# Pairs of tiles in the prefix counts, weights by head at unit ends, and loads, copies and transposes moved between queues and engines in a four-layer graph kernel

## The chip, the cores and the metric

The kernel runs on one core of one Trainium2 chip. The metric is the time of one execution on the device in microseconds (us), the median of the runs shown. The core has these engines: PE (matrix products, with its weight loads shown as PEld), DVE (vector), ACT (scalar functions), POOL (GpSimd), and SP, which only issues transfers. Each engine works off its own instructions in order. Transfers are issued from queues of SP, ACT or POOL and run on 16 DMA engines.

## The reference

A graph of 3327 nodes with 512 features passes through four layers. After each one, x becomes the layer norm of x plus the layer's result. Layers 0, 2 and 3 are graph attention, with 8, 8 and 4 heads; layer 1 takes the mean over the first 64 neighbours of each row.

```python
# attention (layer 0; layers 2 and 3 the same with an elu behind)
Wh = einsum('ni,hio->hno', h, W);  f1 = Wh . a1;  f2 = Wh . a2
e  = leaky_relu(f1[:, :, None] + f2[:, None, :], 0.2)
attention = softmax(where(adj > 0, e, -9e15), axis=-1)
h_prime = einsum('hnm,hmo->hno', attention, Wh)
# layer 1 (sage)
keep    = (A > 0) & (cumsum(A > 0, axis=1) <= 64)
nb_mean = keep @ X / max(keep.sum(1), 1)
out     = leaky_relu(X @ W_line.T + b_line) + where(cnt > 0, leaky_relu(nb_mean @ W_nb.T + b_nb), 0)
```

## The kernel before

Nodes are cut into NT = 26 tiles of 128. The transposed adjacency lies in on-chip memory as `mask`, one byte per entry, 128 x 26 x 3328. The instructions of PE are in the order in which they are written; those of the other engines are ordered by a planner, except where `tc.keep_in_program_order` pins one.

**Projection.** For each tile, `project1` transposes x on PE and `project2` multiplies with the weights, which yields the values and, in 2H extra columns, f1 and f2. ACT copies these to `fc` (L269), DVE scales the values (L271), and they go to DRAM as `v`. In layer 0 the projection runs beside the loading of the mask: 104 pieces of up to 416 KB (`mask_steps`), of which `EARLY` = 88 are loaded and set here and the rest in the first units of attention. `prepare` (L293) and `cut` (L317) turn f1 and f2 of one half of the tiles into exponentials, rows in DRAM (`rd`) and bf16 pieces; for the second half they are jobs of the first attention unit.

**Attention.** A softmax weight is a maximum of two products of exponentials, so a weight tile `t` is one DVE instruction: the larger of a row `rb` and a column, times the mask (L402). ACT makes from it an fp8 tile `y` that tells which side won (L405). PE multiplies `t` with the values into four accumulators `po` (L411) and `y` and the mask with small coefficient columns into `pd`, the denominators (L371). Target nodes go in two halves of 1664 columns, heads in NS = 4 slots: a `unit` (L358) is one half and one slot, with HS = 2 heads in layers 0 and 2 and one in layer 3, and loops over the 26 source tiles j:

```python
for k, h in enumerate(heads):
    t = tp.tile([P, IW], F32, name="t")          # 3 * HS buffers
    nc.vector.scalar_tensor_tensor(t, rb[k], self.qc[:, j, h:h + 1], ...)
```

Rows come by POOL's queue (L350, a pool of 3 buffers, so one row of the next unit can come early and the other only after a row of this unit was last read), values `vj` by SP's queue, two tiles at a time, in four buffers. At a unit's end `po` is copied to `ob`, its first part by DVE (L429) and three by ACT (L427). PE transposes `ob` in four groups of up to four blocks (`transposed`, L435) during the next unit, one job per j; each group is copied to `hb` (by ACT, in layer 3 by DVE, L443) and stored to `hd` on SP's queue. After the last slot of a half `pd` is copied to `db` (L458 ACT, L459 DVE); the job `reciprocals` sums it on PE (L466) and divides on DVE (L474 to L477).

**Between layers** `finish` loads rows of `hd` (SP's queue) and of the layer's input (POOL's queue), two tiles at a time, and does division, sum and norm; the first two tiles come before the next layer's loop (`ending`).

**Sage.** A first part (L623, L626) multiplies each tile with two weight matrices. In the second part, target nodes go in 13 blocks of 256. For each block and each of the 26 source tiles `kept` makes the tile `kt`: ACT copies the count carried in from the tiles before into a PSUM tile (`carry_in`, L694), PE adds the running count inside the tile by a triangular matrix (L702), DVE compares with 64 and multiplies with the mask (L706). There are two such PSUM tiles, 128 x 256 each. PE then adds three products per source tile into `acc` (L734); while one block is summed the `kt` of the next are made, up to 11 tiles ahead. Carries come as `cy`, four tiles at a time, by POOL's queue (L592). Finished tiles are normed (ACT: square root, identity) and projected for layer 2 (ACT: exponential).

**Layer 3's second half** holds its output in `g` and does elu, statistics and norm as slots end (`final`), with the last of it behind the last unit.

## Time and profile before

| | |
|---|---|
| median of 3 runs | 3477.88 us (3473.75 to 3479.80) |
| profiled execution, its own time | 3476.22 us |
| span of its instructions | 3474.4 us |
| mean clock granted to PE | 0.983 |
| busy: PE, DVE, ACT, POOL | 3320.6, 2699.8, 2387.0, 213.3 us |
| L402 (weight tiles, DVE) | 1040 instructions, 1944 ns each |
| L405 (ACT) | 1040, 1766 ns each |
| L706, L694, L702 (prefix counts) | 338 each: 420, 374, 273 ns |

| stage | from, about (us) |
|---|---|
| projection of layer 0, mask loads | 0 |
| attention of layer 0, 8 units | 156 |
| sage, first part; second part | 985; 1190 |
| attention of layer 2, 8 units | 1820 |
| projection of layer 3 | 2615 |
| attention of layer 3, 8 units; its end | 2765; 3440 |

Lengths of single instructions overlap at their ends: back to back, instructions start closer together than the length of one, so a rate is read from starts. A time line's row gives start, length (of a group of neighbours), engine, line, tiles and, in brackets, the idle time before it and what ended it. A row of the waits gives who waited for what, total us, times, longest.

### The profile page before, as it was taken

The numbers are of one execution on the slowest core, as the hardware profiler recorded it, in microseconds if no ns is written. First come the engines' busy times: TensorE is split into PE (matmuls) and PEld (weight loads), VectorE is DVE, ScalarE is ACT, GpSimd is POOL, SyncE is SP. The second block draws the span as 40 slices with busy tenths as digits, with TensorE's granted clock in tenths as the row PEclk, the third lists the DMA queues.
The fourth block names the chain that finished last, engine by engine and source line by source line (L and its number), as shares of the span: only waits on it lengthen the run. The fifth ranks groups of instructions, "written<-read, shape, count | busy, mean of one in ns | idle before, by whom it ended". The sixth has DMA issues, their size and how long they took to land.

```text
span 3474.4 us, 48117 instructions
## 1 busy us (share of the span) xinstructions
PE 3320.6 (96%) x18873; PEld 1700.4 (49%) x18926; DVE 2699.8 (78%) x2771; ACT 2387.0 (69%) x2324; POOL 213.3 (6%) x340
## 2 busy tenths in 40 slices
PE   8799999999989999999989999999998999999997
PEld 6544444444444455545554444444446655555553
DVE  6699999999957544344349999999997766668886
ACT  1388988999953343443328999899997655558885
POOL 3100000000010111111110000000001000000000
PEclk9899999999989999999999999999999999999998
DMA  9722111110133422222220111111106511112211
GB/s 382 284 86 68 50 48 47 47 49 28 37 121 122 136 82 68 75 67 69 73 78 18 48 49 47 51 46 43 39 28 205 176 33 44 40 46 91 83 37 47
DMA packets 205354, 276.67 MB, mean 80 GB/s; under 512 B 19325, under 2 KB 140359, under 8 KB 205128
## 3 DMA queue, kind: packets, MB, share of 16 engines
q1 hardware_dynamic: 173464, 164.97, 14.5%
q0 software_dynamic: 26720, 102.65, 9.3%
q10 hardware_dynamic: 4944, 5.98, 0.5%
q8 instruction: 149, 2.44, 0.3%
q14 instruction: 77, 0.63, 0.1%
HBM read 204.92 MB, written 68.60 MB: 79 GB/s over the span
## 4 chain that ended last, share of the span: by engine, by line
PE 59%; issue 27%; DVE 6%; DMA 5%; ACT 2%; POOL 1%; ACTq 0%; POOLq 0%; SPq 0%; DVEq 0%
PE po L411 33%; PE acc L734 9%; PE pd L371 4%; PE pw L265 4%; DVE t L402 3%; DMA raw<-in_adjT_dram 3%; PE pz L623 3%; PE pi L626 2%; PE pt L435 1%; ACT y L405 1%; DMA cy<-ctd 1%; PE pk L702 1%; DVE kt L706 1%; PE pe L466 1%; PE pt L254 1%
## 5 line engine op out<-in xcount | busy, mean ns | idle before, releaser
L402 DVE SCALAR_TENSOR_TENSOR t<-rb,qc,mask 128x1664 f32<-128x1664 f32 x1040 | 1959.5, 1944 | 191.7 <-PE po L411 154.4
L405 ACT ACTIVATE y<-t,bi,sc 128x1664 fp8e4<-128x1664 f32 x1040 | 1771.6, 1766 | 339.1 <-PE pd L371 324.5
L411 PE MATMUL po<-t,vj 128*64 128x448 f32 (+3 forms) x8320 | 1934.8, 521 | 23.8 <-DVE t L402 23.5
L411 PEld LDWEIGHTS po<-t,vj 128*64 128x64 f32 (+1 forms) x8320 | 856.4, 148 | 972.8 <-issue 676.3
L734 PE MATMUL acc<-zs,kt 128*128 128x512 bf16 x1314 | 394.7, 380 | 1.5
L265 PE MATMUL pw<-wsb,xT 128*128 128x264 f32 (+1 forms) x1248 | 301.8, 397 | 18.6 <-DVE vt L271 15.6
L734 PEld LDWEIGHTS <-kt 128*128 128x128 fp8e4 x2028 | 198.2, 98 | 226.4 <-issue 29.8
L694 ACT CAST pk<-cy 128x256 f32<-128x256 bf16 x338 | 124.0, 374 | 268.2 <-DVE kt L706 220.5
L265 PEld LDWEIGHTS pw<-wsb,xT 128*128 128x128 f32 x1248 | 240.7, 197 | 62.9 <-issue 14.1
L371 PE MATMUL pd<-y,sden 128*32 128x448 fp8e4 (+1 forms) x4160 | 259.7, 342 | 10.5 <-ACT y L405 10.5
L706 DVE SCALAR_TENSOR_TENSOR kt<-pk,mask 128x256 fp8e4<-128x256 f32 x338 | 140.8, 420 | 157.2 <-PE pk L702 156.6
L734 PE MATMUL acc<-zl,kt 128*128 128x512 bf16 x661 | 251.1, 380 | 1.4 <-DMA zl<-zd 0.8
L371 PEld LDWEIGHTS <-sden 128*32 128x32 bf16 x4160 | 117.7, 96 | 162.4 <-issue 139.7
L269 ACT COPY fc<-pw 128x8 f32<-128x8 f32 (+1 forms) x156 | 23.6, 162 | 148.2 <-PE pw L265 148.2
L271 DVE TENSOR_TENSOR vt<-pw,dc 128x256 f32<-128x256 f32 x156 | 58.7, 417 | 80.8 <-ACT dc L266 76.6
L350 POOL DMA_DIRECT2D rb<-r x40 | 21.2, 532 | 1617.0 <-DVE t L402 1610.2
L702 PE MATMUL pk<-mask,upto 128*128 128x256 fp8e4 x338 | 92.3, 273 | 19.9 <-ACT pk L694 18.9
L526 DVE TENSOR_SCALAR mask<-raw 128x832 fp8e4<-128x832 int32 (+2 forms) x98 | 58.4, 603 | 51.0 <-DMA raw<-in_adjT_dram 50.7
L623 PE MATMUL pz<-wn,xT 128*128 128x512 f32 x208 | 96.1, 606 | 1.3 <-ACT xT L617 1.3
L626 PE MATMUL pi<-wl,xT 128*128 128x512 f32 x208 | 93.5, 592 | 0.0
L592 POOL DMA_DIRECT2D cy<-ctd x91 | 67.8, 745 | 395.9 <-ACT pk L694 267.8
L714 DVE SCALAR_TENSOR_TENSOR y<-acc,cnt,bnb 128x512 f32<-128x512 f32 x26 | 19.5, 751 | 83.5 <-PE acc L734 83.5
(167 smaller groups left out, 1750.7 us busy)
## 6 DMA issues: line engine op xcount, KB each, us to landing
vj<-v SPq DMA_DIRECT2D x312, 128.0 KB
rb<-r POOLq DMA_DIRECT2D x40, 832.0 KB, 4.7
raw<-in_adjT_dram SPq DMA_DIRECT2D x71, 416.0 KB
cy<-ctd POOLq DMA_DIRECT2D x78, 256.0 KB, 3.9
h<-hd SPq DMA_DIRECT2D x65, 256.0 KB
hd<-hb SPq DMA_DIRECT2D x60, 256.0 KB
v<-vt SPq DMA_DIRECT2D x50, 256.0 KB
xr<-x POOLq DMA_DIRECT2D x45, 256.0 KB, 3.2
```

Source lines behind the costliest of these rows:

```text
L265: nc.tensor.matmul(pw[e][:, :FW + H], xT[:, c, :], wsb[:, c, e, :], start=c == 0, stop=c == FC - 1)
L371: nc.tensor.matmul(pd[c][32 * kk:32 * kk + 32, :w_], lhsT, rhs, start=(kk, c) not in seen, skip_group_check=final is not None, stop=last a ...
L402: nc.vector.scalar_tensor_tensor(t, rb[k], self.qc[:, j, h:h + 1], mask[:, j, i0:i0 + IW], op0=ALU.max, op1=ALU.mult)
L405: nc.scalar.activation(y, t, AF.Sigmoid, bias=self.bi[:, j, h:h + 1], scale=self.sc[:, j, h:h + 1], saturate=False)
L411: nc.tensor.matmul(po[c][k * D:(k + 1) * D, :z - a_], vj[:, j % 2, k * D:(k + 1) * D], ts[k][:, a_:z], start=j == 0, stop=j == NT - 1)
L592: nc.gpsimd.dma_start(out=cy[:, :n, :], in_=ctd[t:t + n, b * GW:(b + 1) * GW] .rearrange("(o t) i -> o t i", o=1).to_broadcast([P, n, GW]))
L623: nc.tensor.matmul(pz, xT[:, c, :], wn[:, c, :], start=c == 0, stop=c == FC - 1)
L626: nc.tensor.matmul(pi, xT[:, c, :], wl[:, c, :], start=c == 0, stop=c == FC - 1)
L694: nc.scalar.copy(pks[k % 2], carry[b, t // 4 * 4][:, t % 4, :])
L702: nc.tensor.matmul(pk, upto, mask[:, t, i0:i0 + GW], start=False, stop=True, skip_group_check=True)
L706: nc.vector.scalar_tensor_tensor(kt, pk, NEIGHBOURS, mask[:, t, i0:i0 + GW], op0=ALU.is_le, op1=ALU.mult, saturate=False)
L734: nc.tensor.matmul(acc, kts[t][:, s * P:(s + 1) * P], zs(t, c) if c < 2 else zl[:, t, :], start=t == 0 and c == 0, stop=t == NT - 1 and c ...
```

## The change

- `kept` makes two tiles at a time: PSUM tiles of 128 x 2 x 256, one matmul, one ACT copy, one DVE instruction for both; `kt` has half as many buffers of twice the size.
- In units with two heads the weights of the first two and of the last two source tiles are made head by head: (0,0), (1,0), (0,1), (1,1).
- `fc` is gone: f1 and f2 are copied into `rc` and `qc` and worked on in place.
- In layers 0 and 2 all copies of `po` and `pd` are ACT's.
- In layer 3's first half DVE transposes 32 x 32 blocks from PSUM into `ob`, and four transfers per unit put the blocks in place in DRAM, in runs of 32 numbers; the transposes on PE and the copies to `hb` fall away there.
- `reciprocals` is cut in two jobs, the sums on PE and, two tiles later, the division; at the very end the first transposes go ahead of the sums, and tiles are normed and stored in reverse.
- `prepare` and `cut` of the second half come two tiles later in layers 0 and 2, and instructions of theirs are pinned to program order.
- The first `finish` in the loops behind layers 0 and 2 (tiles 2 and 3) loads `hd` by POOL's queue.
- `EARLY` is 82, the first 8 mask pieces (not 4) are issued by ACT's queue, and w0's transposed rows have four buffers instead of three.

```diff
-    def finish_steps(pool, xin, layer, t0, n, hbufs=6):
+    def finish_steps(pool, xin, layer, t0, n, hbufs=6, eng=nc.sync):
...
-                load_tile(h, hd, t, nc.sync)
+                load_tile(h, hd, t, eng)
...
         def columns(self, pool):
...
-            self.fc = pool.tile([P, NT, 2 * H], F32, name=f"fc{li}")
...
-                nc.scalar.copy(self.fc[:, t, e * H:(e + 1) * H], pw[e][:, FW:FW + H])
+                nc.scalar.copy((self.rc, self.qc)[e][:, t, :], pw[e][:, FW:FW + H])
...
-        def prepare(self, pool, half, tag="rr", bufs=2):
+        def prepare(self, pool, half, tag="rr", bufs=2, pinned=False):
...
-            f1, f2 = self.fc[:, ts, :H], self.fc[:, ts, H:]
...
-            nc.vector.tensor_scalar(rc, f1, RCLAMP, -RCLAMP, op0=ALU.min, op1=ALU.max)
+            ins = nc.vector.tensor_scalar(rc, rc, RCLAMP, -RCLAMP, op0=ALU.min, op1=ALU.max)
+            if pinned:
+                tc.keep_in_program_order(ins)
...
-            nc.scalar.activation(qc, f2, AF.Exp, scale=1.0 - ALPHA)
+            nc.scalar.activation(qc, qc, AF.Exp, scale=1.0 - ALPHA)
...
-        def cut(self, pool, half, tag="pc", bufs=1):
+        def cut(self, pool, half, tag="pc", bufs=1, pinned=False):
...
-                nc.vector.tensor_copy(pc[:, :, :, c0], dc)
+                ins = nc.vector.tensor_copy(pc[:, :, :, c0], dc)
+                if pinned:
+                    tc.keep_in_program_order(ins)
...
+            def weights(j, k):
+                h = heads[k]
+                t = tp.tile([P, IW], F32, name="t")
+                nc.vector.scalar_tensor_tensor(t, rb[k], self.qc[:, j, h:h + 1],
+                                               mask[:, j, i0:i0 + IW], op0=ALU.max, op1=ALU.mult)
+                y = yp.tile([P, IW], F8, name="y")
+                nc.scalar.activation(y, t, AF.Sigmoid, bias=self.bi[:, j, h:h + 1],
+                                     scale=self.sc[:, j, h:h + 1], saturate=False)
+                return t, y
...
+                if HS == 1 or j not in (1, NT - 1):
+                    made = {}
+                    for k in range(HS):
+                        for j_ in (j, j + 1) if HS > 1 and j in (0, NT - 2) else (j,):
+                            made[j_, k] = weights(j_, k)
+                ts, ys = zip(*(made[j, k] for k in range(HS)))
...
+            by_dma = HS == 1 and not final
...
-                if c:
+                if by_dma:
...
+                    nc.vector.transpose(ob[:, a_:z], po[c][:, :z - a_])
+                elif c or HS == 2:
...
-                    final(s, s0, n, pt)
-                    return
+                    return final(s, s0, n, pt)
...
-                if HS == 2:
-                    nc.scalar.copy(hb[:, :n], pt[:, :n])
-                else:
-                    nc.vector.tensor_copy(hb[:, :n], pt[:, :n])
+                nc.scalar.copy(hb[:, :n], pt[:, :n])
...
-            for s0, n in QUADS:
-                jobs += [lambda s0=s0, n=n: transposed(s0, n), nothing]
+            if by_dma:
+                for b in range(4):
+                    nc.sync.dma_start(out=hd[i0:i0 + IW, s * P + 32 * b:s * P + 32 * b + 32]
+                                      .rearrange("(q i) f -> i q f", i=32),
+                                      in_=ob[32 * b:32 * b + 32, :].rearrange("p (q f) -> p q f", f=32))
+            else:
+                for s0, n in QUADS:
+                    jobs += [lambda s0=s0, n=n: transposed(s0, n), nothing]
...
-                nc.vector.tensor_copy(db[64:, c * (WB // 2):(c + 1) * (WB // 2)], pd[c][64:, :WB // 2])
...
-            def reciprocals():
-                pe = qp.tile([P, HALF, 2, H], F32, name="pe", tag="q")
+                (nc.scalar.copy if HS == 2 else nc.vector.tensor_copy)(
+                    db[64:, c * (WB // 2):(c + 1) * (WB // 2)], pd[c][64:, :WB // 2])
+            held = []
...
+            def sums():
...
+                pe = po[0][:, :2 * HALF * H].rearrange("p (q o h) -> p q o h", q=HALF, o=2) if final and s == NS - 1 else \
+                    qp.tile([P, HALF, 2, H], F32, name="pe", tag="q")
+                held.append(pe)
...
+            def reciprocals():
+                pe = held[0]
...
-                    nc.vector.tensor_tensor(r_[:, :, k, ss], pv[:, :, 0, k, ss], rc[:, :, k, ss], op=ALU.mult)
+                    tc.keep_in_program_order(
+                        nc.vector.tensor_tensor(r_[:, :, k, ss], pv[:, :, 0, k, ss], rc[:, :, k, ss], op=ALU.mult))
...
-            return jobs[:2] + [reciprocals] + jobs[2:]
+            if final and s == NS - 1:
...
+                take = []
+                return [lambda: take.append(transposed(*QUADS[0])), lambda: take.append(transposed(*QUADS[1])),
+                        sums, reciprocals] + [lambda q=q: take[q]() for q in range(2)] + \
+                    [lambda q=q: transposed(*q)() for q in QUADS[2:]]
+            return jobs[:2] + [sums, nothing, reciprocals] + jobs[2:]
...
-                    ys, ahead = ahead, finish(fp, xin, prev, t0 + 2, 2) if t0 + 2 < NT else None
+                    ys, ahead = ahead, finish(fp, xin, prev, t0 + 2, 2, 6, nc.sync if t0 else nc.gpsimd) \
+                        if t0 + 2 < NT else None
...
-                    tc.tile_pool(name="sb_k", bufs=NT + 10, reuse_waits="tile") as kp, \
+                    tc.tile_pool(name="sb_k", bufs=NT // 2 + 5, reuse_waits="tile") as kp, \
...
-                pks = [pkp.tile([P, GW], F32, name=f"pk{i}") for i in range(2)]
+                pks = [pkp.tile([P, 2, GW], F32, name=f"pk{i}") for i in range(2)]
...
-                    nc.tensor.matmul(pk, upto, mask[:, 0, :GW], start=True, stop=True)
...
-                order = [(b, t) for b in range(len(blocks)) for t in range(NT)]
+                    nc.tensor.matmul(pk, upto, mask[:, 0:2, :GW], start=True, stop=True)
...
+                order = [(b, t) for b in range(len(blocks)) for t in range(0, NT, 2)]
...
                 def carry_in(k):
...
-                        nc.scalar.copy(pks[k % 2], carry[b, t // 4 * 4][:, t % 4, :])
+                        nc.scalar.copy(pks[k % 2], carry[b, t // 4 * 4][:, t % 4:t % 4 + 2, :])
...
                 def kept(b, t):
...
-                    nc.tensor.matmul(pk, upto, mask[:, t, i0:i0 + GW], start=False, stop=True,
+                    nc.tensor.matmul(pk, upto, mask[:, t:t + 2, i0:i0 + GW], start=False, stop=True,
...
-                    kt = kp.tile([P, GW], F8, name="kt")
-                    nc.vector.scalar_tensor_tensor(kt, pk, NEIGHBOURS, mask[:, t, i0:i0 + GW],
+                    kt = kp.tile([P, 2, GW], F8, name="kt")
+                    nc.vector.scalar_tensor_tensor(kt, pk, NEIGHBOURS, mask[:, t:t + 2, i0:i0 + GW],
...
-                    return kt
+                    return [kt[:, 0, :], kt[:, 1, :]]
...
                 def output(acc, t):
...
-                kts = [kept(0, t) for t in range(4)]
+                kts = kept(0, 0) + kept(0, 2)
...
-                            if b == 0 and len(kts) < NT:
-                                kts.append(kept(0, len(kts)))
+                            if b == 0 and len(kts) < NT and t % 2 == 0:
+                                kts += kept(0, len(kts))
...
-                            if not last and (len(ahead) < 10 and t % 2 == 1 and b > 0 if s == 0 else
-                                             len(ahead) < min(NT, t + 11)):
-                                ahead.append(kept(b + 1, len(ahead)))
+                            if not last and (len(ahead) < 10 and t % 4 == 1 and b > 0 if s == 0 else
+                                             len(ahead) < min(NT, t + 10) and t % 2 == 1):
+                                ahead += kept(b + 1, len(ahead))
...
-                    ys, ahead = ahead, finish(fp, x2, L2, t0 + 2, 2) if t0 + 2 < NT else None
+                    ys, ahead = ahead, finish(fp, x2, L2, t0 + 2, 2, 6, nc.sync if t0 else nc.gpsimd) \
+                        if t0 + 2 < NT else None
...
+                    def take():
+                        h = fp.tile([P, 4, P], F32, name="h", bufs=2)
+                        nc.vector.tensor_tensor(h[:, :n], pt[:, :n], rec[:, HALF + q0:HALF + q0 + n, s:s + 1]
...
+                        if s == NS - 1:
...
+                        return take
+                    take()
...
-                    for q in range(qs.start, qs.stop):
+                    for q in reversed(range(qs.start, qs.stop)):
...
+        L0.columns(cp)
...
-            L0.columns(wp)
...
-            EARLY = 3 * NT + 10
-            msteps = mask_steps(rw0, pieces[:EARLY], 5, (), False, 4)
+            EARLY = 3 * NT + 4
+            msteps = mask_steps(rw0, pieces[:EARLY], 5, (), False, 8)
...
             def attend(pool, tag, dst, wT, a, k, held):
...
-                wt = pool.tile([P, F], F32, name="wt", tag=tag)
+                wt = pool.tile([P, F], F32, name="wt", tag=tag, bufs=FC if tag == "wt" else 1)
...
-                return [lambda: L0.prepare(f0, 1, "xr", 1), lambda: L0.cut(f0, 1, "h", 2)] + count_jobs(pool, 0)
+                return [lambda: None] * 2 + [lambda: L0.prepare(f0, 1, "xr", 1, True), lambda: L0.cut(f0, 1, "h", 2, True)] + \
+                    count_jobs(pool, 0)
...
-                L2.attention(rp, lambda pool, half, s: [lambda: L2.prepare(mp, 1, "rr", 1), lambda: L2.cut(mp, 1, "pc", 1)]
+                L2.attention(rp, lambda pool, half, s: [lambda: None] * 2 +
+                             [lambda: L2.prepare(mp, 1, "rr", 1, True), lambda: L2.cut(mp, 1, "pc", 1, True)]
...
```

## The prediction

> **What bounds the kernel now.** First I read slices and windows, to cut the run into stages; then, stage by stage, the time line and the table of waits, to see what each stage is paced by.
>
> From the page, busy tenths in 40 slices of 87 us (PE, DVE, clock granted to PE, DMA):
>
> ```profile
> PE   8799999999989999999989999999998999999997
> DVE  6699999999957544344349999999997766668886
> PEclk9899999999989999999999999999999999999998
> DMA  9722111110133422222220111111106511112211
> ```
>
> PE looks full everywhere, so it can't be what tells the stages apart. The others do: DMA fills only the start (to about 155 us, the projection of layer 0 with the mask loads); DVE is full from 160 to 970 (attention, layer 0) and from 1820 to 2612 (layer 2); only PE is full in the sage layer (985 to 1820) and in layer 3's attention (2765 to 3440).
>
> The time line inside layer 2 (start, length, engine, line):
>
> ```profile
> 1898.68 24.30 DVE L402 SCALAR_TENSOR_TENSOR t<-rb,qc,mask 128x1664 f32<-128x1664 f32 x13
> 1903.11 13.47 ACT L405 ACTIVATE y<-t,bi,sc 128x1664 fp8e4<-128x1664 f32 x8 [1.44 <-PE pd L371]
> 1922.89 0.62 DVE L429 COPY ob<-po 128x448 f32<-128x448 f32 x1
> 1923.88 28.02 DVE L402 SCALAR_TENSOR_TENSOR t<-rb,qc,mask 128x1664 f32<-128x1664 f32 x15 [0.37 <-DMA rb<-r]
> ```
>
> DVE makes a weight tile each 24.30/13 = 1.87 us with nothing between; 52 of them are 97.1 us, and a unit is 98. The rest of a unit is the copy (0.62) and the wait for the next rows (0.37). ACT needs 13.47/8 = 1.68 each, 87.6 a unit, with 8 copies of about 0.5 some 92. PE needs 13 pairs of tiles at 5.83 (32 instructions, where they run unpaced in the chain) and 0.87 for the denominators, 87.1, about 2.8 for the masks' denominators and 1.9 for transposes: 92. So DVE sets these 16 units with 5 us to spare on both others, and only what DVE loses counts there.
>
> The waits of DVE, first in layer 0 (160 to 985), then in layer 2 (1820 to 2615): total, times, longest:
>
> ```profile
> DVE t L402 <- DMA rb<-r: 3.2, 4, 1.6
> DVE rec L474 <- PE pe L466: 2.7, 1, 2.7
> ...
> DVE t L402 <- DMA rb<-r: 2.5, 4, 0.8
> DVE rec L474 <- PE pe L466: 2.4, 1, 2.4
> ```
>
> The sage layer's second part (1190 to 1820): PE waits for ACT's carry copies, by the table of waits and by one place on the time line:
>
> ```profile
> PE pk L702 <- ACT pk L694: 18.9, 20, 1.9
> ...
> 1319.37 1.28 ACT L154 ACT_TABLE_LOAD   x1
> 1319.94 0.38 PE L734 MATMUL acc<-zl,kt 128*128 128x512 bf16 x1
> 1321.28 0.27 PE L702 MATMUL pk<-mask,upto 128*128 128x256 fp8e4 x1 [0.96 <-ACT pk L694]
> ```
>
> Start to start that is 1.34 us where 0.215 is normal: a table load on ACT holds up the one tile of lead.
>
> Two more places: the end of layer 0, and a transpose in layer 3.
>
> ```profile
> 992.28 2.77 SPq L126 DMA_DIRECT2D h<-hd  x6
> 1005.25 1.12 PE L615 MATMUL pt<-ident,h 128*128 128x128 f32 x4 [5.75 <-ACT h L161]
> ...
> 2857.63 0.60 PE L435 MATMUL pt<-ident,ob 128*128 128x128 f32 x4
> 2858.06 2.96 PE L411 MATMUL po<-t,vj 128*128 128x448 f32 x8
> ```
>
> **The change, part by part.** The sum is against the profiled execution's own time, 3476.22 us (span 3474.4 and 1.8 around it), 1.7 under the median 3477.88.
>
> *Start.* Six mask pieces of 416 KB leave the DMA-bound start: 2.56 MB at the 370 to 390 GB/s of its rows is 6.7 us. They come back in layer 0's first units, 3 on ACT, 3 on DVE at 0.59: +1.8. A fourth buffer for w0's transposed rows and four more raw loads on ACT's queue move bytes about in a full DMA: 0. Pinning the second half's preparation takes some 7 us of small DVE work from before the first weight tile (156.0) to after it; DVE is full there, so 0 net. It also puts its two Exp between Sigmoids: two table loads of 1.28 on ACT (cover: ACT's 5 us a unit), and PE, in written order, waits at the preparation's transposes for clamp and Exp. DVE has six tiles of lead, 11 us. Before, 3.5 us of DVE idle already came of such a PE stop, so from 0 to 5. Take -5; ends -7 and +3.
>
> *Attention, layers 0 and 2.* Seven first copies of ob that stand between units on DVE: 7 x 0.61 = 4.3; db of the half in the middle 1.1; the reciprocals' wait 2.7 and 2.4, since the sums now run two tiles earlier; the rows' wait 3.2 and 2.5, since a head's rows come free 4 tiles (7.5 us) before their successor is read, not 2 (3.7), against 4.7 to landing. That is 11.3 and 10.3. The copies go to ACT: +0.5 a unit, within its 5. The new order makes PE start tile pair 0 one DVE instruction later and end 1.1 us later: covered by six tiles of lead inside a stage. The lead is tightest at tile (3,1), which reuses (1,0): by the durations above about 1.3 us remain. If that cover is gone, 1 to 2 us a unit go back, 16 units. Preparation as above costs layer 2 the same 0 to 5. Take -9 and -9; ends -11 and +4 each.
>
> *Boundaries.* Tiles 2 and 3 of hd are from half 0 and long written; SP takes their loads behind the last unit's stores (988 to 992), which wait for ACT. On POOL they stand behind wn, wl, blb and cy and can go at about 981, with landing 2.9 to 3.2 us like its neighbours xr. PE's 5.75 wait goes, and with it part of a cold stretch (the next 8 matmuls take 6.0 us, not 3.7). Behind them POOL has only xr of the same tiles, 0.5 us each. Against it: the later end of PE (1.1) and four db copies in series on ACT. Take -5; ends -7 and +1. At 2612 those six loads went out early already, so there only the later end counts: +1.
>
> *A page that speaks against it.* The row: POOL's xr loads land 2.9 us after issue beside DVE work. The Trainium skill, "SBUF — State Buffer", section "Who interferes with whom", says that descriptors made on GpSimd are shut out while DVE runs a two-port mode, 620 ns becoming 3100. By that, an estimate, two loads lose 5 us and the boundary is worth 0; by the row, -5.
>
> *Sage, second part.* PE streams the same columns (0.108 us for 256, so 0.215 for 512): 0. ACT's copies halve in number: 338 x 374 ns = 126 us become 169 x about 0.58 = 98; DVE's 142 become about 117. Neither bounds. What counts is lead: a pair buys 1.5 us a step instead of 0.76, so a 1.6 us ACT block that stopped PE for 1.1 stops it for 0.3 or so. Of 18.9 us, plus some 4 us of stops too short for the table, I take half: -11. Ends: -17, and +4 if the first block starts later because two wide tiles have to be there first.
>
> *Layer 3.* A unit's transposes cost PE 0.43 three times and 0.12 (2857.63 to 2858.06 and so on): 1.4, four units, 5.6, PE-bound: all gain. DVE loses four copies of 0.68 and one of ob, gains four block transposes, for which the nearest row is the PSUM copy, 0.61 and 0.56; it is 60% busy. Of po, PE needs c at 0.75 us steps, and DVE frees it each 0.6. The stores become 6656 runs of 128 B a unit instead of 1664 of 512 B. The trace has no such run; queue q1's mean packet takes 14.5% of 16 x 3474 over 173464, 46 ns, so 19 us a unit on 16 engines, on SP's queue among the vj loads. These have four buffers of 6.3 us, 25 us. Hidden up to 60 ns a run. Take -5; ends -5.6 and, at 70 ns a run (4 us over, four times), +12.
>
> *The page on it.* The Trainium skill, "DMA: Bandwidth & Descriptors", section "Specifications", wants 512 B for line rate and says less is read, modified and written. Were that to double the 46 ns, an estimate, stores would take 38 us a unit, 13 too long: +52, not -5, and the whole slower. No run here shows it yet.
>
> *Tail.* Transposes fill PE's 1.1 us wait, the reciprocals come 0.6 later, the odd last tile is stored before others: -1; ends -2 and +2.
>
> f1 and f2 in place: same instructions, 0; it could add a wait only where the halves were taken as one tile.
>
> Sum: -5 -9 -9 -5 +1 -11 -5 -1 = -44: **3432 us**.
>
> **The rivals.**
> *The covers are thinner.* ACT gets Exp, copies and masks in the units where it was 92 of 98, and PE's in-order stops reach DVE: layers 0 and 2 give back 5 to 10 each, 3442 to 3452. For: 3.5 us of stop at 175. Against: 5 us to spare a unit.
> *Sage's stops stay* because ACT's table loads, not the tile count, make them, or another engine is late next (DVE's kt, now 0.7): +11, 3443. With the former, about 3460.
> *Slower:* the 128 B stores choke vj. Loss is 4 x (6656 X / 16 - 25); it eats the other 39 us at X = 84 ns a run, and at 100 the time is 3437 + 66 = 3503. For: nothing so short was ever in this queue in number. Against: 46 ns is the mean at 950 B, and a shorter run should not cost more.
> *It does not do what it says:* only PE follows the written order; the planner may place DVE's and ACT's work as before, and the rows' 5.7 and the copies' gain fall out: 3440.
>
> **How the numbers follow.** Forecast with its ends (3412 to 3440) 0.60; covers or sage or planner, one or two together (3440 to 3470) 0.28; within 0.2% 0.03; slower 0.09, nearly all from the stores. What a measurement of this kernel can tell from no change is 0.2%, 7 us: faster means under 3471. The range, 3405 to 3469, reaches 7 under the forecast's own for more cold-clock gain and takes in the second case; it leaves out the 0.12 and a few hundredths below.
>
> **What would show it.** First weight tile at 145 to 151; unit pitch in layers 0 and 2 of 97.1 to 97.5 with no L429 on DVE and no rb waits; the PE wait at the second part of layer 0's boundary gone; pk waits under 10 us; layer 3's half 0 at 81.3 a unit, not 82.7. Wrong if po waits for vj (128 B runs over 60 ns), if t waits for po or y in units 0, or if POOL's h loads land after 992.

## The result and the profile after

The changed kernel takes 3432.3 us (median of 4 runs, 3426.0 to 3434.5) beside 3478.3 for the kernel before (3473.8 to 3479.8, 4 runs): a ratio of 0.9867 with a 95% interval of 0.985 to 0.9884. The forecast was 3432.0. The two profiled executions, 3476.2 and 3434.5 us, lie 41.8 apart, where the forecast's terms add up to 44.

The busy tenths of the page (PE, DVE, the clock granted to PE, DMA), now in slices of 86 us:

```profile
PE   8799999999999899999989999999998999999997
DVE  5799999999967443434349999999997766668876
PEclk9999999999999999999999999999998999999998
DMA  9732111111043422222220111111116411112211
```

Nothing but lengths has moved, so the gain has to be read by stage, between marks that both time lines show. The table gives the two profiles of the kernel before (the second comes from the experiments), the profile after, and the spread over those experiments that leave the stage's code as changed. All in us.

| stage | before | after | others | change | forecast |
|---|---|---|---|---|---|
| start to the first weight tile `t` | 156.0, 154.8 | 149.7 | 144.4 to 147.2 | -6.3 | -5 |
| layer 0, first to last `t` | 813.5, 812.8 | 803.6 | 803.9 to 805.2 | -9.9 | -9 |
| last `t` to the first carry product `pk` | 220.9, 218.8 | 213.8 | 213.6 to 215.7 | -7.0 | -5 |
| sage layer, first `pk` to last `acc` | 609.3, 612.7 | 599.9 | 597.7 to 600.9 | -9.4 | -11 |
| last `acc` to the first `t` of layer 2 | 20.0, 19.0 | 20.4 | 19.2 to 20.6 | +0.4 | 0 |
| layer 2, first to last `t` | 792.7, 792.5 | 781.9 | 780.2 to 781.1 | -10.8 | -9 |
| last `t` of layer 2 to the first of layer 3 | 137.7, 137.8 | 143.1 | 141.3 to 146.5 | +5.4 | +1 |
| layer 3 from there to the last store that POOL issues | 715.5, 715.6 | 711.4 | 709.3 to 713.8 | -4.1 | -6 |

From POOL's last store to the end of the span it is another 9.0 us before and 8.5 after, so that to the very end layer 3 changed by -4.6. The way out of layer 2 takes back half of that layer's gain: from its first `t` to the first of layer 3 it is 930.4 and 930.3 before, 925.0 after.

Layer 2 at a unit's end, by the time line (start, length, engine, line), first DVE and then ACT:

```profile
1884.75 28.02 DVE L398 SCALAR_TENSOR_TENSOR t<-rb,qc,mask 128x1664 f32<-128x1664 f32 x15
...
1891.38 1.69 ACT L441 COPY ob<-po 128x448 f32<-128x448 f32 x4
1893.08 5.10 ACT L401 ACTIVATE y<-t,bi,sc 128x1664 fp8e4<-128x1664 f32 x3
```

DVE goes from one unit into the next without the copy and without a wait. From first `t` to first `t` the units without other work take 96.85, where they took 97.85 to 98.1; the forecast's sign was 97.1 to 97.5. The table of DVE's waits, layer 0 and then layer 2 (total, times, longest), has lost the lines for `rb` and for `rec`; none of the waits for `po` and `y` that are left falls into a layer's first unit:

```profile
DVE t L398 <- PE po L421: 1.7, 3, 0.6
DVE t L398 <- ACT y L401: 1.3, 4, 0.6
DVE mask L558 <- DMA raw<-in_adjT_dram: 0.2, 1, 0.2
...
DVE t L398 <- PE po L421: 1.4, 1, 1.4
```

The sage layer's second part, PE's waits. The first line stood at 18.9 in 20 waits; the second, for a transfer, at 0.8:

```profile
PE pk L735 <- ACT pk L727: 7.4, 5, 4.5
PE acc L767 <- DMA zl<-zd: 4.6, 1, 4.6
```

The end of layer 0, POOL's queue and then PE:

```profile
961.92 0.55 POOL L126 DMA_DIRECT2D h<-hd  x1
...
962.99 0.54 POOL L126 DMA_DIRECT2D h<-hd  x1
...
972.97 1.75 PE L647 MATMUL pt<-ident,h 128*128 128x128 f32 x8
975.87 3.70 PE L655 MATMUL pz<-wn,xT 128*128 128x512 f32 x8 [1.16 <-ACT xT L649]
...
984.85 0.66 PE L647 MATMUL pt<-ident,h 128*128 128x128 f32 x4 [1.84 <-ACT h L161]
```

The wait of 5.75 for ACT's `h` is 1.84 now, and the eight products behind it take 3.6 us instead of 6.0.

Layer 3's first half, one unit's `ob` by its tile (durations in ns: least, median, most):

```profile
L439 DVE STREAM_TRANSPOSE ob<-po x4: 539/573/642, 2809.2 to 2810.8; 128x448 f32<-128x448 f32 x2, 128x384 f32<-128x384 f32 x2
L461 SPq DMA_DIRECT2D hd<-ob x4: 336/825/2748, 2811.4 to 2815.3; - x4
```

A block transpose of 128x448 takes about what the copy took that it replaces (618). From PE's first `po` product of a unit to that of the next (a unit's pitch, from here on), the three units that used to hold a predecessor's transposes take 81.24 each in this half, for 82.67.

### The profile page after: what moved, and what is told of

It reads as the page before. It is cut to its first block, busy times and chain, and to the rows that moved or that the text cites. A ratio compares the mean times of both kernels' runs of the same rounds, so it can differ in the third digit from the quotient of the medians.

```text
span 3432.3 us, 47383 instructions
## 1 busy us (share of the span) xinstructions
PE 3295.2 (96%) x18705; PEld 1656.3 (48%) x18705; DVE 2666.0 (78%) x2571; ACT 2374.3 (69%) x2172; POOL 215.1 (6%) x344
## 4 chain that ended last, share of the span: by engine, by line
PE 73%; issue 12%; DMA 6%; DVE 4%; ACT 3%; POOL 1%; SPq 0%; POOLq 0%; ACTq 0%; DVEq 0%
PE po L421 49%; PE pd L373 7%; PE acc L767 5%; DVE t L398 3%; PE pw L264 3%; PE pz L655 3%; PE pi L658 3%; DMA raw<-in_adjT_dram 2%; DMA cy<-ctd 2%; ACT y L401 1%; PE pt L449 1%; PE pe L487 1%; DMA r<-rr 0%; POOL cy L624 0%; PE pa L966 0%
## 5 line engine op out<-in xcount | busy, mean ns | idle before, releaser
L421 PE MATMUL po<-t,vj 128*64 128x448 f32 (+3 forms) x8320 | 1912.8, 521 | 24.4 <-DVE t L398 24.2
L421 PEld LDWEIGHTS po<-t,vj 128*64 128x64 f32 (+1 forms) x8320 | 835.0, 148 | 978.1 <-issue 710.6
L767 PE MATMUL acc<-zs,kt 128*128 128x512 bf16 x1352 | 404.7, 381 | 0.0
L727 ACT CAST pk<-cy 128x512 f32<-128x512 bf16 x169 | 98.4, 587 | 287.1 <-DVE kt L739 234.0
L739 DVE SCALAR_TENSOR_TENSOR kt<-pk,mask 128x512 fp8e4<-128x512 f32 x169 | 116.2, 688 | 108.2 <-PE pk L735 107.8
L268 ACT COPY rc<-pw 128x8 f32<-128x8 f32 (+1 forms) x78 | 12.7, 163 | 151.0 <-PE pw L264 151.0
L256 DVE TENSOR_REDUCE xsum<-xT 128x4 f32<-128x512 f32 x78 | 53.0, 681 | 39.7 <-ACT xT L255 39.3
```

Of the source, the lines that this page charges most:

```text
L421: nc.tensor.matmul(po[c][k * D:(k + 1) * D, :z - a_], vj[:, j % 2, k * D:(k + 1) * D], ts[k][:, a_:z], start=j == 0, stop=j == NT - 1)
L727: nc.scalar.copy(pks[k % 2], carry[b, t // 4 * 4][:, t % 4:t % 4 + 2, :])
L739: nc.vector.scalar_tensor_tensor(kt, pk, NEIGHBOURS, mask[:, t:t + 2, i0:i0 + GW], op0=ALU.is_le, op1=ALU.mult, saturate=False)
L767: nc.tensor.matmul(acc, kts[t][:, s * P:(s + 1) * P], zs(t, c) if c < 2 else zl[:, t, :], start=t == 0 and c == 0, stop=t == NT - 1 and c ...
```

## The experiments

The kernel before ran beside each group of them, at medians of 3471.3, 3474.6 and 3476.5; wholes are therefore given as ratios to it, and the readings are taken from stage lengths.

### Copies back on VectorE

```diff
-                elif c or HS == 2:
+                elif c:
...
-                (nc.scalar.copy if HS == 2 else nc.vector.tensor_copy)(
+                nc.vector.tensor_copy(
```

> The change with the first copy of ob and the two lower copies of db on VectorE again in layers 0 and 2. Theory (a copy between units on VectorE is paid in full, 0.61 us each): unit pitch of 96.1, 96.85 and 97.6 up by 0.6, each layer's attention up by 5.4 (803.6 and 804.8 to 809 to 810; 780 to 782 to 786 to 787), whole 3438 to 3444. Rival 1 (ScalarE's extra copies delay its sigmoids, and with them gone the lost time comes back): attention within 2 us of the change. Rival 2 (VectorE waits for rows come back and the planner fills the gaps with the first tile's work, as in the kernel with the plain order): attention up by 8 or more, the stretch to layer 3's first projection product down by 5 or more.

Layer 0's attention is 809.0, layer 2's 787.7: 3.8 to 5.4 and 5.8 to 7.5 more than with the copies on ACT. From first `t` to first `t`, units without other work take 97.6 throughout. Ratio 0.9918 (0.9903 to 0.9933). The groups of DVE in layer 2 (busy us, mean ns, idle before):

```profile
L443 DVE COPY ob<-po 128x448 f32<-128x448 f32 x7 | 4.4, 624 | 0.9
...
L475 DVE COPY db<-pd 64x384 f32<-64x384 f32 x2 | 1.0, 557 | 0.0
```

That is 5.4 of busy time and 0.9 of idle time before it: the theory's price. No wait for `rb` appeared, so rival 2 is out.

### Plain order of the weight tiles

```diff
-                if HS == 1 or j not in (1, NT - 1):
-                    made = {}
-                    for k in range(HS):
-                        for j_ in (j, j + 1) if HS > 1 and j in (0, NT - 2) else (j,):
-                            made[j_, k] = weights(j_, k)
+                made = {(j, k): weights(j, k) for k in range(HS)}
```

> The change with the weight tiles made and used by tile and then by head at every j, as before, the copies of ob and db and the jobs left as changed. Theory (the new order at unit ends buys the rows' time to land): VectorE waits for rb come back, 3.2 us in layer 0 and 2.5 in layer 2, each layer's attention longer by 2.5 to 3.5, whole 3437 to 3439. Rival 1 (the copies moved to ScalarE alone hid the wait, or the planner moved VectorE's instructions anyway): no rb waits, whole 3431 to 3434. Rival 2 (the order costs TensorE what it buys VectorE): whole below 3430.

Layer 0's attention is 813.5 and layer 2's 788.7; ratio 0.9927 (0.9915 to 0.9939). The rows' waits are back, in layer 0:

```profile
DVE t L398 <- DMA rb<-r: 4.1, 3, 2.2
```

But the order is worth 8.3 to 9.9 us in layer 0 and 6.8 to 8.5 in layer 2, not the 3.2 and 2.5 that the rows' waits of the kernel before had put on it. DVE's time in the two layers, taken from start to start, says where the rest goes. Beside the changed kernel, DVE is idle 5.9 us longer in layer 0 and 2.9 in layer 2, and in each 3.8 us more are work of the next stage, which the planner puts there and which is paid here and not later; in layer 2 (time line, DVE):

```profile
2388.34 0.69 DVE L191 SCALAR_TENSOR_TENSOR xr<-e,xr 128x512 f32<-128x512 f32 x1
2389.06 0.69 DVE L192 SCALAR_TENSOR_TENSOR h<-h,xr 128x512 f32<-128x512 f32 x1
...
2486.53 0.67 DVE L191 SCALAR_TENSOR_TENSOR xr<-e,xr 128x512 f32<-128x512 f32 x1
```

Layer 0 is as long here as in the kernel before (813.5 and 813.1), though DVE's copies are gone. That does not say that the copies are worth nothing without the order: beside the kernel before, DVE has 5.0 us of copies and 2.8 of idle time less, but 5.3 of mask pieces and pinned work more, which the rest of the change moved into this layer, and 1.9 more of the next stage's work. A kernel with copies and order both undone and the rest of the change kept was not run, so whether the two gains add stays open.

### Prefix products of one tile

```diff
-                pks = [pkp.tile([P, 2, GW], F32, name=f"pk{i}") for i in range(2)]
+                pks = [pkp.tile([P, GW], F32, name=f"pk{i}") for i in range(2)]
...
-                order = [(b, t) for b in range(len(blocks)) for t in range(0, NT, 2)]
+                order = [(b, t) for b in range(len(blocks)) for t in range(NT)]
```

> The change with the sage layer's prefix products taken back to one tile each (carry copy, product and comparison of 256 columns, 338 of them), all else as changed. Theory (the pair's longer lead is what shortened the second part): the second part goes from 598.7 back to about 608, PE's waits for pk from 7.4 to about 19 us, the copies and comparisons to 338 each; whole about 3442 (+9.5). Rival (the second part was shortened by something else, such as other work that the planner put elsewhere, or the cold clock): second part stays at 598 to 601, whole 3432 to 3434.

The second part is 612.4, 11.5 to 14.6 longer; ratio 0.9925 (0.9912 to 0.9937). PE's waits and ACT's copies by their tile:

```profile
PE pk L735 <- ACT pk L727: 19.3, 20, 2.1
```

```profile
L727 ACT CAST pk<-cy x338: 357/376/383, 1166.9 to 1729.7; 128x256 f32<-128x256 bf16 x169
```

The old waits (18.9) are back, and no wait for `zl` is left; it stands at 3.8 to 4.9 in every other profile with pairs. The pair does it. That it does so by its lead fits the waits, and ACT's and DVE's saved time should lie on neither path, since both sat idle for most of this part. But the waits are not all of it: beside the kernel with the loads on SyncE's queue (the next section), whose second part is 13.4 shorter, PE's idle time makes 8.0 (25.6 and 17.6, all gaps), and most of the rest is that the 2028 products into `acc` start closer together (449.7 us from start to start, and 442.9). Why they do was not followed.

### Boundary loads on SyncE's queue

```diff
-                    ys, ahead = ahead, finish(fp, xin, prev, t0 + 2, 2, 6, nc.sync if t0 else nc.gpsimd) \
+                    ys, ahead = ahead, finish(fp, xin, prev, t0 + 2, 2, 6, nc.sync) \
...
-                    ys, ahead = ahead, finish(fp, x2, L2, t0 + 2, 2, 6, nc.sync if t0 else nc.gpsimd) \
+                    ys, ahead = ahead, finish(fp, x2, L2, t0 + 2, 2, 6, nc.sync) \
```

> The change with the loads of hd's tiles 2 and 3 on SyncE's queue again at both boundaries. Theory A (GpSimd's queue is what gained at the end of layer 0 and what lost at the end of layer 2, by letting three Exp ahead of the Sqrt of tiles 0 and 1): from the last t of layer 0 to the first carry product, 215.0 us, +5 to +7; from the last t of layer 2 to the first projection product of layer 3, 25.5 us, back to 18 to 20; whole 3431 to 3434. Theory B (the queue gained at the end of layer 0, but the loss at the end of layer 2 comes from the early work on tile 0 that no longer finds gaps in layer 2's attention): +5 to +7 at the first, 25 to 26 still at the second; whole 3437 to 3440. Theory C (the queue does nothing): both within 1 us, whole 3431 to 3434 with the first still at 215.

From the last `t` of layer 0 to the first carry product it is 214.0 (213.8 with GpSimd's queue), and the second boundary is 144.3 (143.1), with its first product at 23.8 (25.5). Ratio 0.9874 (0.9859 to 0.9889). That is theory C, the queue does nothing, with 1.2 between the two at the second boundary, where the kernels with the change spread over 5. SP's queue at the end of layer 0 tells why:

```profile
958.52 3.03 SPq L126 DMA_DIRECT2D h<-hd  x6
969.66 5.95 SPq L454 DMA_DIRECT2D hd<-hb  x4
```

Before, the same six loads stood behind the four stores (992.28 after 988.04). In this kernel the planner puts them ahead of the stores on SP itself. What the two kernels have in common is that the loads go out before the stores, and with this program around it that no longer needs another queue. That this is what gained is read from the rows; no run has the loads behind the stores with the rest of the change kept. On POOL they were in fact slow: a median of 9.0 us to landing, in a queue with 1 MB each of `wn` and `wl`, not the 2.9 of the forecast's row, and still early enough.

### The first tiles of layer 2's output early

```diff
-                             if (half, s) == (0, 0) else [],
-                             ending=lambda: ends.extend(finish(f2, x2, L2, 0, 2, 2)))
+                             if (half, s) == (0, 0) else [lambda: None] * 2 + early() if (half, s) == (1, 2) else [])
```

`early()` returns the steps of `finish_steps(f2, x2, L2, 0, 2, 2)` as jobs, and a last one that hands the tiles on.

> The change with the division, ELU and norm of the first two row tiles of layer 2's output written into the unit of half 1, strip 2, instead of after the last unit. Theory A (the projection of layer 3 starts late, 24 to 25.5 us after the last weight tile where it was 19.1, because VectorE has no gaps left in layer 2 into which the work of the first tile used to fall): the first projection product comes 8 to 18 us after the last weight tile; VectorE pays for it inside the attention, some 8 instructions of 0.68 us, 781 to 785 to 788; from the last weight tile of layer 2 to the first of layer 3, 141 to 146 now, 6 to 12 less if the first tile sets it. Rival B (the four Exp that ScalarE runs ahead of the first Sqrt do it, whatever was made early): first product still at 22 or later. Rival C (the projection's later tiles set its end): first product early, but still 139 to 146 to layer 3's first weight tile, and the whole 3 to 6 longer than the change.

This is about the one stage that the change made longer. In the kernel before, the time line shows part of the first tile's work inside layer 2's attention, in DVE's gaps (L180 at 2320.56, L191 at 2418.55, L192 at 2516.60); in the kernel after there are no gaps, and nothing of it is done before the last `t`. Before, ACT's `rs` and `h` and the first products then stand 8.9 to 19.1 us after the last `t` (2612.26):

```profile
2621.20 0.30 ACT L154 ACTIVATE rs<-mv,eps 128x2 f32<-128x2 f32 x1
2626.39 1.52 ACT L161 ACTIVATE h<-h,rs 128x512 f32<-128x512 f32 x2
2628.86 1.51 PE L254 MATMUL pt<-ident,h 128*128 128x128 f32 x6
...
2631.33 5.93 PE L265 MATMUL pw<-wsb,xT 128*128 128x260 f32 x16 [0.54 <-ACT xT L256]
```

After, they stand 19.6 to 25.5 after it (2569.33):

```profile
2588.94 0.29 ACT L154 ACTIVATE rs<-mv,eps 128x2 f32<-128x2 f32 x1
...
2591.24 1.50 ACT L161 ACTIVATE h<-h,rs 128x512 f32<-128x512 f32 x2
2592.09 1.97 PE L253 MATMUL pt<-ident,h 128*128 128x128 f32 x8 [3.93 <-ACT h L161]
...
2594.87 5.44 PE L264 MATMUL pw<-wsb,xT 128*128 128x260 f32 x14 [0.82 <-ACT xT L255]
```

With the first two tiles made early, the first product comes 17.8 after the last `t` (2569.66):

```profile
2585.71 1.94 PE L253 MATMUL pt<-ident,h 128*128 128x128 f32 x8
2587.48 2.75 PE L264 MATMUL pw<-wsb,xT 128*128 128x260 f32 x8
...
2595.59 0.95 PE L253 MATMUL pt<-ident,h 128*128 128x128 f32 x4 [3.61 <-ACT h L161]
```

So A holds for the first product: the missing early work is what made it late, and the third tile too comes at 25.9 as before (26.0) and not at 31.2. It does not hold for the stage. The stretch to layer 3's first weight tile is 146.9, the attention grew by 4 to 6 (785.9), and the ratio is 0.9902 (0.9885 to 0.9918): rival C decides. The kernel with the plain order says the same: six such instructions in its gaps, where the kernel before had three, and the first product at 18.3, but a stretch of 141.4.

Nor is the late start what the changed kernel loses. The transposes of the seventh tile start 47.9 us after the last `t` before, behind a stop of 5.9 for ACT's `h`, and 47.8 after: by then the two are level. From there to the first `t` of layer 3 it is 89.8 before (90.3 in its second profile) and 95.3 after. Over the whole stretch PE's idle time is 18.4 before and 21.8 after, and its busy time 119.2 and 121.3; the largest wait, before and then after:

```profile
PE pt L254 <- ACT h L161: 7.8, 3, 5.9
```

```profile
PE pt L253 <- ACT h L161: 13.6, 5, 3.9
```

PE needs 3.95 us a tile in this projection, 103 for 26, and with the first tiles made early the stops for ACT and DVE merely fell elsewhere.

### The kernel before, once more

> The kernel before, unchanged, profiled a second time. It tells how far a stage's length moves from one profile to the next. If the loss between layers 2 and 3 is real, the stretch from the last weight tile of layer 2 to the first of layer 3 is 136 to 140 again (137.7 before; 141.3 to 146.9 in the kernels with the change); if it is a matter of the run, it is 141 or more. If the change shortens the start, the first weight tile comes at 150 to 156 (156.0 before; 144.4 to 149.7 with the change); if that was the chip, at 144 to 148.

The stretch is 137.8 (137.7 in the first profile), and the other stages lie within 3.4 us. The loss at this boundary is real. The first weight tile comes at 154.8.

### Groups of four tiles into layer 3

```diff
-                for t0 in range(0, NT, 2):
-                    ys, ahead = ahead, finish(fp, x2, L2, t0 + 2, 2, 6, nc.sync if t0 else nc.gpsimd) \
-                        if t0 + 2 < NT else None
+                t0 = 0
+                while t0 < NT:
+                    ys, n1 = ahead, t0 + len(ahead)
+                    ahead = finish(fp, x2, L2, n1, min(4, NT - n1), 10, nc.sync if t0 else nc.gpsimd) if n1 < NT else None
```

> The change with layer 2's output finished (division, ELU, norm) in groups of four row tiles instead of two on the way into layer 3's projection, with the buffers for it. It halves the alternation of Exp and Sqrt on ScalarE: some 14 table loads of 1.28 us between the last weight tile of layer 2 and the first of layer 3 instead of 25 to 27. Theory D (TensorE's 21 to 25 us of waits in this stretch, mostly for ScalarE's norm, come of those table loads): stretch from 141 to 147 down to 128 to 136, whole 3412 to 3422, faster than the change. Rival E (the stretch is set by round trips between TensorE, ScalarE and VectorE in the projection itself and by the clock that falls when TensorE stops): 139 to 146, whole as the change. Rival F (groups of four make the first products wait longer): first product 3 to 6 later, stretch 145 to 152.

15 table loads instead of 27 in the stretch, but 145.2 us; the first product at 26.4. Ratio 0.9866 (0.9839 to 0.9894), as the change. The total is what rival E said, but a mark in the middle shows two effects that cancel. The seventh tile's transposes start at 57.6, ten us later than in the profile after (47.8): groups of four make the early tiles wait, as rival F has it, though not the first product. From there on it is 87.5 us, for 95.3 in the profile after and 95.0 to 102.0 in the other kernels with the change. So fewer table loads, or fewer and larger groups, may well be worth some 8 us behind the seventh tile; E is not shown, and the two were not told apart.

What sets the later stops of this projection stays open. The mean granted clock over the stretch is 0.93 and 0.91 in the two profiles of the kernel before, which are equally long, and 0.88 to 0.92 in the kernels with the change; whether the clock makes the stops longer or the stops the clock lower was not told apart.

### PE transposes in layer 3

```diff
-            by_dma = HS == 1 and not final
+            by_dma = False
...
-                nc.scalar.copy(hb[:, :n], pt[:, :n])
+                if HS == 2:
+                    nc.scalar.copy(hb[:, :n], pt[:, :n])
+                else:
+                    nc.vector.tensor_copy(hb[:, :n], pt[:, :n])
```

> The change with layer 3's first half transposed by TensorE again (four products and a VectorE copy for each group, one store of 512 B runs instead of four of 128 B). Theory (the block transposes took 1.43 us a unit from TensorE and the short runs are hidden): unit pitch in the first half from 81.2 to 82.7, whole +5.6, about 3438. Rival (the short stores, or ScalarE and VectorE's new work, gave it back in the second half: (1,0) and (1,2) were 0.9 and 2.6 longer than before): first half +1.4 a unit, second half shorter by 2 to 4, whole 3433 to 3436.

The pitch is 82.67 three times, as before: 1.43 a unit. Layer 3 to POOL's last store is 717.6 (711.4). Ratio 0.9886 (0.9873 to 0.99): some 6.5 us over the change's 0.9867, 4 over the 0.9874 of the kernel above whose loads are on SyncE's queue, which ran beside it; the intervals overlap, so it is the pitch that tells. The theory holds, and the second half did not get shorter (348.4, after 345.5): the short stores take nothing back. Of those 2.9 us the first unit of that half has all: it holds the fourth unit's transposes, and its granted clock was 0.96 against 0.98.

### Strips stored four times

```diff
-                for b in range(4):
+                for b in (0, 1, 2, 3) * 4:
                     nc.sync.dma_start(out=hd[i0
```

The same data are written again.

> The change with each of the four strip stores of layer 3's first half issued four times over (26624 runs of 128 B a unit instead of 6656). The changed kernel's trace has these runs at about 16 ns of an engine each, and the four stores land in some 10 us. Theory (the vj loads behind them have about 25 us of cover, and the loss is the stores' time over 25 us): 40 us a unit, 13 to 17 too long, three or four times, so unit pitch in the first half from 81.2 to 94 to 98 and the whole 45 to 65 longer. Rival (the queue lets the vj loads pass between the stores, so that short runs never choke them): pitch 81.2 to 83, whole within 5 us. If the loss is far above the theory's, the forecast's hidden limit of 60 ns a run was too high.

The pitch is 84.2, 86.2, 87.2 instead of 81.2 three times; layer 3's attention is 13.9 longer. Ratio 0.9921 (0.9907 to 0.9936). PE's waits in this half:

```profile
PE po L421 <- DMA vj<-v: 9.5, 3, 3.5
```

The mechanism of the slower rival is there: the loads of `vj` stand behind the stores. The price is not. The DMA view of a unit, with 26624 short runs among its 30204 packets (85 us, 16 engines), and of a unit of the changed kernel (81 us):

```profile
q1 hardware_dynamic: 30204, 5.01, 34.1%
```

```profile
q1 hardware_dynamic: 10256, 2.56, 14.5%
```

34.1% of 16 x 85 us over 30204 packets is 15 ns each. In the packet records of the changed kernel's trace a run of 128 B takes 14.1 ns in the mean, one of 512 B 27.6. By the forecast's own formula, a loss of 4.7 us a unit (the mean of three) as 26624 X / 16 - 25 gives X = 18 ns. Not all of that loss need be waiting: the waits add up to 9.5 of 13.9, and behind the two of over 3 us the clock granted to PE fell to 0.5, for 3.4 and 6.8 us. By the waits alone X is 17 ns. I had expected 40 us of stores from the 10 us in which one set lands, and that was too much; that part of the 10 is latency, which four sets pay once, would explain it but was not measured. At 17 to 18 ns the changed kernel's 6656 runs take some 7 us of the 25 that cover them.

### The old start

```diff
-            EARLY = 3 * NT + 4
-            msteps = mask_steps(rw0, pieces[:EARLY], 5, (), False, 8)
+            EARLY = 3 * NT + 10
+            msteps = mask_steps(rw0, pieces[:EARLY], 5, (), False, 4)
...
-                wt = pool.tile([P, F], F32, name="wt", tag=tag, bufs=FC if tag == "wt" else 1)
+                wt = pool.tile([P, F], F32, name="wt", tag=tag)
```

> The change with the start of before: six more mask pieces ahead of layer 0's attention, four raw loads on ScalarE's queue instead of eight, one buffer for the transposed rows of all weights. Theory (2.56 MB fewer bytes in a start that the DMA bounds are worth 6.7 us, of which the six mask pieces cost 1.8 in layer 0): first weight tile 144 to 148 later by 5 to 7, layer 0's attention shorter by 2 to 3, whole 3 to 5 longer. Rival (the start is not paced by bytes but by the projection, so the pieces were hidden): first weight tile within 1.5 us, whole the same or 1 to 2 shorter.

The first weight tile comes at 152.6. In a window over the start (last columns: PE's clock, DMA share, GB/s), this kernel and then the one with groups of four, whose start is the changed one:

```profile
0.00:152.61 152.61, 123.18 (x581) 103.59 (x581) 94.88 (x202) 31.48 (x116) 47.73 (x81) 0.99 1.00 375
```

```profile
0.00:145.72 145.72, 124.84 (x581) 103.86 (x581) 90.64 (x196) 31.34 (x116) 47.37 (x80) 0.98 1.00 375
```

Both at 375 GB/s, and 6.9 us apart: 57.2 and 54.6 MB, the 2.56 MB of the forecast at its price of 6.7. The two kernels first profiled ran at 367 and 365 GB/s, so the same bytes took 156.0 and 149.7. Layer 0's attention did not get shorter as expected (806.4; 803.6 to 805.2 with the change). DVE does set ten pieces there instead of thirteen, 1.5 us less from start to start, but it waits 7.9 us instead of 3.2 (for `po` 3.6 and 1.7, for `y` 2.1 and 1.3, for pieces 1.7 and 0.2). Why it waits more was not followed. Ratio 0.988 (0.9854 to 0.9906).

### No pins

```diff
-                return [lambda: None] * 2 + [lambda: L0.prepare(f0, 1, "xr", 1, True), lambda: L0.cut(f0, 1, "h", 2, True)] + \
+                return [lambda: L0.prepare(f0, 1, "xr", 1), lambda: L0.cut(f0, 1, "h", 2)] + \
...
-                L2.attention(rp, lambda pool, half, s: [lambda: None] * 2 +
-                             [lambda: L2.prepare(mp, 1, "rr", 1, True), lambda: L2.cut(mp, 1, "pc", 1, True)]
+                L2.attention(rp, lambda pool, half, s: [lambda: L2.prepare(mp, 1, "rr", 1), lambda: L2.cut(mp, 1, "pc", 1)]
```

> The change with the preparation and cut of the second half left to the planner in layers 0 and 2 as before (not pinned, no two empty jobs ahead). Theory (the pins move some 7 us of VectorE's small work from before the first weight tile to after it, net nothing): start longer by 4 to 7, layer 0's attention shorter by as much, whole within 2 us; layer 2 within 2 us. Rival 1 (the pins bought the start, since its end waits for that work and TensorE's stop of 3.5 us at 175 comes back): whole 4 to 8 longer. Rival 2 (the pins cost layer 2 its gaps): layer 2's attention 2 to 4 shorter, whole shorter.

Layer 0's attention has 7.3 us less of DVE's small work by lengths (24.1 for 31.4), 4.5 from start to start, which is what counts, and is yet 805.1, since a stop for `po` of 5.8 us comes at 170, as 3.5 did before. Layer 2's is 781.9. The start, 149.4, ran at 367 GB/s, which by its bytes alone makes 149. So the pins move some 4 us behind the first tile, not 7, and save a stop of about that size: net nothing in those stages. Ratio 0.9885 (0.9862 to 0.9908), too wide to tell from the change's.

### Sums and reciprocals in one job

```diff
-            return jobs[:2] + [sums, nothing, reciprocals] + jobs[2:]
+            return jobs[:2] + [lambda: (sums(), reciprocals())] + jobs[2:]
```

> The change with the sums of the denominators and their reciprocals in one job again, in all layers. Theory: VectorE waits for the sums again, 2.7 us in layer 0 and 2.4 in layer 2, of which some may be covered; in layer 3's second half, where the split put everything behind it two tiles later, the unit after strip 1 goes back from 88.2 to about 85.6, so layer 3 gains 2.6; whole about 2 to 3 longer than the change. Rival 1 (the split is what made the unit after strip 1 longer, and the wait is hidden in layers 0 and 2): whole 2 to 3 shorter. Rival 2 (the split does nothing for layer 3): whole 4 to 6 longer, that unit still 88.

Layer 0's attention is 806.8 (1.6 to 3.2 more), layer 2's 782.4 (0.5 to 2.2 more), and DVE waits again, in layer 0:

```profile
DVE rec L500 <- PE pe L487: 1.9, 1, 1.9
```

In layer 2 it is 1.2. Before they were 2.7 and 2.4. The unit of layer 3 that was to go back from 88.2 to 85.6 did not: rival 2. By the pitch there was nothing to take back, since that unit, the third of the second half, takes 85.4 in the kernel before, in the one after and here; the 88.2 came of a mark that the split moves. Ratio 0.9895 (0.988 to 0.9909).

None of these versions beats the change by more than the runs can tell.

## Why the prediction was right

*Start, -5: -6.3 measured, -6.9 at equal rates.* The bytes were priced rightly (6.7). Of the deductions, the three more pieces do cost DVE 1.5 us in layer 0, though no run shows that layer shorter without them; the stop on PE that I had allowed for went away with the pins.

*Attention, -9 and -9: -9.9 and -10.8.* The list of copies, sums and rows was right as a sum and wrong as a list. Undone one at a time, the copies cost 3.8 to 5.4 and 5.8 to 7.5 (forecast 5.4 each), the sums 1.6 to 3.2 and 0.5 to 2.2 (2.7 and 2.4), the order 8.3 to 9.9 and 6.8 to 8.5 (3.2 and 2.5). In layer 2 that is 13.1 at the least for a gain of 12.4 at the most, so they do not add there. That before, the copy lay in time in which the row was awaited anyway would explain it; it is argued, not shown. The 7 us of pinned work were a sum of lengths, and some 4 from start to start. That the planner might undo the order (the rival that it does not do what it says) was wrong: no wait for `rb` is left. ACT's cover held, with the four copies in 1.69 us; so the thin covers fell.

*End of layer 0, -5: -7.0.* The wait of 5.75 went as written, to 1.84, and with it part of the cold stretch. POOL's queue was not needed for it: the loads go out ahead of the stores on SP's queue as well. On the page that spoke against it (the Trainium skill, "SBUF — State Buffer", section "Who interferes with whom"): POOL's issues took 0.54 us each here, and no starved one is seen, but these fall after DVE's weight tiles have ended. POOL's 40 issues of `rb`, in the middle of the weight tiles, took 0.53 to 0.62. Whether any DVE instruction here is of the kind that the rule is about, no run shows.

*Sage, second part, -11: -9.4, and 11.5 to 14.6 when undone.* The waits went from 18.9 to 7.4 as half of them were to; but the one for `zl` went from 0.8 to 4.6, which I had not named. The stops too short for the table, put at some 4 us, are there as well: most of what the waits do not explain is the closer spacing of the products.

*Layer 2 to layer 3, +1: +5.4.* The step that failed: "At 2612 those six loads went out early already, so there only the later end counts: +1." It put everything behind the first tiles at nothing. What the runs showed is that PE's waits for ACT's `h` in this stretch went from 7.8 us to 13.6, and that the loss arises behind the seventh tile. The queue of the loads is not the cause (144.3 with SyncE's). The step also overlooked that DVE's gaps in layer 2, which the change closes, were where the planner had put part of the first tile's work; that made the first product 6.4 us late, but putting it back left the stretch at 146.9. What causes the 5.4 stays open.

*Layer 3, -5, and tail, -1: -4.1 together, -4.6 to the end of the span.* 1.43 a unit came in all three pitches of the half. The fourth unit's share falls into the first unit of the second half: 89.06 at a granted clock of 1.00 in four profiles, against 90.30 before at the same clock, but 90.76 at 0.98 in the profile after. What the clock took there is the difference. The fear of 128 B runs was answered by 14.1 ns a run: the break-even at 84 ns and even the hidden limit of 60 were far. A nearer row than the queue's mean of 46 ns was at hand: in the packet records of the kernel before, 113192 runs of 512 B on that queue took 27.7 ns each. That trace does have 48 runs of 128 B, at 214 ns each, but on POOL's queue (84 ns in the profile after). The rule weighed there (the Trainium skill, "DMA: Bandwidth & Descriptors", section "Specifications", 512 B for line rate) is right in that a byte cost twice as much in such runs, 14.1 ns for 128 B against 27.6 for 512; the doubling of a run's time, the +52 worked out from it, did not come.

The total fell on the forecast because errors cancelled, and by luck: the end of layer 0 came out 2.0 better, layer 2's attention 1.8, the start 1.3 and layer 0's attention 0.9; the boundary behind layer 2 was 4.4 worse, layer 3 with the tail 1.9, the sage layer 1.6 and the way from it 0.4. That leaves 2.3, and the profiled execution is indeed 2.4 over 3432; that the median of the runs lies 0.3 from it is chance.

## What to carry to other kernels

Where a planner fills gaps, list what stands in a gap before pricing its removal: work that was done there comes back at the end of the stage. Then read at a later mark whether it costs anything: here the first product came 6.4 us later and the seventh tile did not. Two edits to the same gap are priced together, and to learn whether they add takes the kernel with both undone. A total that stands still may hide two effects that cancel, as in the groups of four; a mark in the middle tells. For short stores on a queue with loads behind them, compare the stores' time with the cover of the buffers; the size of a run matters only when that is near.

## What the runs showed of the hardware

**Behind a block of narrow products the clock fell, in some runs.** The first unit of layer 3's second half has the same PE instructions in eleven of the twelve kernels with the change, but took 89.1 us at a granted clock of 1.00 (four of them), 90.7 to 90.8 at 0.98 (six) or 92.4 at 0.96 (one). In the kernel with copies on VectorE (92.4), 26 products of 8 columns take 3.43 us, and the eight wide ones behind them 5.89, 0.74 each:

```profile
3070.86 3.43 PE L487 MATMUL pe<-c1w,db 128*128 128x8 f32 x26
3074.14 5.89 PE L421 MATMUL po<-t,vj 128*128 128x448 f32 x8
```

Windows over these places (the third column from the end is PE's clock), of that kernel and then of the one with the plain order, where the unit took 89.1:

```profile
3070.00:3075.00 5.00, 5.00 (x31) 4.23 (x30) 2.84 (x5) 0.00 (x0) 0.20 (x1) 0.82 0.06 15
3075.00:3080.00 5.00, 5.00 (x12) 2.05 (x14) 0.30 (x1) 0.00 (x0) 0.00 (x0) 0.50 0.00 0
```

```profile
3075.00:3080.00 5.00, 5.00 (x33) 4.04 (x33) 3.08 (x5) 0.00 (x0) 0.20 (x1) 1.00 0.07 18
3080.00:3085.00 5.00, 5.00 (x28) 2.43 (x28) 1.95 (x1) 2.43 (x2) 0.00 (x0) 1.00 0.11 30
```

PE had no wait in either, and the clock fell to 0.50 in one. In the clock's own record such a fall lasts 3.4 or 6.8 us, and it begins 2.3 to 4.1 us after the block does. It also falls behind a wait: the next unit has one of 1.78 us in all twelve, and in six the clock is 0.50 for 3.4 us behind it. The Trainium skill, "TensorE: Matmul & The Clock Gate", section "Part 1: The HAM clock gate", says that the gate judges by free-running windows of about 3.4 us and closes after an idle one. An undisturbed block takes 2.96 us, less than such a window, so the rule alone does not explain these falls. That products of 8 columns count as little activity is a guess, and no run here tests it.

**The rate of the start differs by run**: 365 to 379 GB/s for the same transfers in the kernels that have the changed start, which took 149.7 to 144.4 us at a DMA share of 0.98 to 1.01.

**A run of 128 B to DRAM** takes 14.1 ns of a DMA engine in the mean, one of 512 B 27.6 (loads and stores together), and four sets of 6656 short runs a unit hold up a queue by 17 to 18 ns a run, over 16 engines.
